# A graph stack of four layers on one core: a rewritten prelude, other buffers for the last turned rows, and attention scores of one head over all 1024 keys

## The chip, the cores and the metric

The kernel runs on one core of a Trainium2 chip. A core has five engines that work at the same time, each through its own list of instructions in order: TensorE (PE; its weight loads are PEld), VectorE (DVE), ScalarE (ACT), GpSimd (POOL), and SyncE (SP), which issues the DMA transfers here. SBUF is the memory on the core, 128 partitions wide; matmuls write to PSUM, which has eight banks of 512 float32 a partition. The metric is the time on the device of one execution, in microseconds; the median of three runs is taken.

## What is computed

x is (16, 1024, 64) float32: 16 elements of 1024 nodes with 64 channels. adj is (16, 1024, 1024), symmetric, zeros and ones, about 1.6% ones, heavier towards the first nodes. Four layers are added to x one after another, each on a normalized copy:

```
h = relu(layernorm(x)); x += quantiles(h, dilate(adj)) -> two-layer MLP
h = relu(layernorm(x)); x += (adj + I) @ h / rowsum(adj + I)
h = relu(layernorm(x)); x += attention(h, adj) @ W_proj.T + b_proj
h = relu(layernorm(x)); x += adj @ (h @ W3) + b3

quantiles: dilate drops every skip-th neighbour of nodes with over 10 neighbours;
           per node and channel, over the remaining neighbours' values:
           .25 q(.25) + .5 q(.5) + .25 q(.75), linear interpolation, plus h itself
attention: 8 heads of 64; q, k, v = h @ W_qkv.T
           g0, g1 = exp(h @ W_gamma.T + b_gamma)
           softmax(g0 * (q @ k.T) / 8 + g1 * adj) @ v
```

## The kernel before

**Layer 0 by ranks.** The kernel never sorts a node's neighbours. It ranks each channel's 1024 values once, and then looks for the wanted order statistic of every node by counting. `ranked` (L942) normalizes two elements, so that 2 x 64 channels fill the 128 partitions, and `ranks` (L542) sorts those 128 rows with 55 compare-exchange steps in float32 (L577 to L579), stores the sorted values to DRAM (`vs_d`), reverses the 55 steps in float16 with masks kept in DRAM (L609 to L612) to get each value's rank, and stores the ranks to DRAM (`rk_d`). `dilate` (L470) makes the thinned neighbour masks of an element. `stages` (L1016) then prepares an element in small steps: it fetches its ranks, builds the neighbour matrix (`neighbours`, L511), the rank positions that are sought (`positions`, L627, ending with six rows `krow` that ScalarE copies), and the table of differences of sorted values (`sorted_table`, L668).

**The comparison loop.** `picks` (L779) has for every element 96 steps: 8 groups of 8 channels, 2 halves of 512 nodes, 6 order statistics. A step (`compare`, L813) is three VectorE passes over 128 x 2048 (`le` L819, `wa` L821, `wb` L823), then matmuls into `prep` and `val` (L842), then `bits` (L854) and `value` (L865). The cumulated counts that it compares come from 512-wide matmuls `px` (L735) whose results ScalarE copies several times (`group`, L713).

**The other layers.** `turned` (L1089) goes once over all 128 blocks of 128 rows of adj: load, row sums on ScalarE, transposes on TensorE (`chunk_cols`, L450), and a store of the transposed block to DRAM (`adjT`). `layer1` (L1104) and `layer3` (L1240) read such blocks back through `turned_rows` (L1099) and multiply with them (`weighted`, L1073). `layer2` (L1123) is the attention: per pair of heads, keys and queries for all nodes (`pk`, `pq`, L1166: each one matmul of 128 output rows for each 512 nodes, copied by ScalarE at L1173, both heads side by side on the partitions), values `pv2`, and then for each of 8 blocks of 128 query nodes:

```
for t in range(NH):                     # half of the keys
    sp[:, 0, :], sp[:, 1, :] = scores of both heads, 512 keys      (L1201)
    for e in range(2):                  # head
        s[e][:, t half] = ad - sp[:, e, :]; nm[e] = its minimum,   (L1210)
                          begun with nm[e] of the first half
exp of each head's 1024 (L406), transposes, eT @ v (L1224), projection (L1233)
```

The minimum is that of the negated scores, so it is the softmax's maximum. One `sp` tile of two PSUM banks exists; matmuls of a tile that are next to each other are held together by `adjoining`.

**What sets the order.** The program is written out in one list. `picks` yields a number after each of its steps, the numbers add up to an account `due`, and as long as the account is above zero the generator `layers()` is advanced, which pays back what each of its steps is worth. A comparison step pays 0.42; a block of `turned` costs 0.3; the three later layers of an element cost 40.3 together. While `picks` works on element b, `background(b + 1)` thins the next element and ranks half of the next pair, one small step for each comparison. Before the first comparison everything of element 0 has to be made: that prelude (`background(0)`, then `els[0].stages`, then the first weights) pays 0.0 for each step up to the end of the ranking and 0.05 for the first group, so that hardly anything of `layers()` lies in it. The prelude runs the ranking and the thinning in turn, two steps of the first for one of the second, and only then the stages of element 0. When `picks` has ended, `alone` is set: the last element's layers 1 to 3 are left, and other buffers are taken for some tiles.

**Constants.** Before all this, L127 to L388 make constant tiles: masks, bit-reversed index tables, selectors, weights. Their scratch memory is given back (L389) just before the pool `sb` is opened (L390), so the first loads of x wait until the last reader of it has gone by.

**Buffers.** `b4`, `b2_`, `a4`, `q4`, `tb` are tiles of SBUF by size class with some buffers each; tag `bt` has 2 buffers, shared by `chunk_cols` and `turned_rows`, `tb` has 6; in PSUM, `pa`, `pb` and `pc_` have 2 banks each.

Of the kernel before, what the change touches and what calls it, by code (L numbers as in the profile page):

```python
# [8 lines left out]
F32 = mybir.dt.float32  # L9
# [29 lines left out]
def tile_preln_adj_stack(  # L39
# [87 lines left out]
    scr_i = sc("scr_i", (P, 5, P), I32)  # L127
    scr_f = sc("scr_f", (P, 3, P))
    identf = const.tile([P, P], F32, name="identf")
    make_identity(nc, identf)  # L130
    ident = const.tile([P, P], HP, name="ident")
    nc.vector.tensor_copy(ident, identf)

    rev_i = sc("rev_i", (P, C), I32)
    nc.gpsimd.iota(rev_i, pattern=[[1, C]], base=0, channel_multiplier=C)
    rev_a = sc("rev_a", (P, C), I32)
    rev_b = sc("rev_b", (P, C), I32)
    nc.vector.memset(rev_a, 0)
    for b_ in range(N.bit_length() - 1):
        up = N.bit_length() - 2 - 2 * b_  # L140
        nc.vector.tensor_scalar(
            rev_b, rev_i, 1 << b_, abs(up), op0=OP.bitwise_and,
            op1=OP.logical_shift_left if up >= 0 else OP.logical_shift_right,
        )
        nc.vector.tensor_tensor(rev_a, rev_a, rev_b, OP.bitwise_or)
    rev = sc("rev", (P, C), HP)
    nc.vector.tensor_copy(rev, rev_a)
    rev_d = dram.tile([P, C], HP, name="rev_d")
    nc.sync.dma_start(rev_d, rev)
    minus_i = const.tile([P, P], BF, name="minus_i")  # L150
    nc.vector.tensor_scalar(minus_i, identf, -1.0, None, op0=OP.mult)
# [3 lines left out]
    fmp_i = scr_i[:, 0, :]  # L155
    nc.gpsimd.iota(fmp_i, pattern=[[1, P]], base=0, channel_multiplier=-1)
    fmp = scr_f[:, 0, :]
    nc.vector.tensor_copy(fmp, fmp_i)


    step2 = sc("step2")
    nc.vector.scalar_tensor_tensor(step2, fmp, 2.0, identf, op0=OP.is_equal, op1=OP.subtract)
    dif = const.tile([P, 2, P], HP, name="dif")
    nc.vector.tensor_scalar(dif[:, 0, :], step2, -SPAN, None, op0=OP.mult)
    nc.vector.tensor_scalar(dif[:, 1, :], step2, -1.0, None, op0=OP.mult)
    less = const.tile([P, 2, P], HP, name="less")
    nc.vector.tensor_scalar(less[:, 0, :], identf, -2.0, None, op0=OP.mult)
    nc.vector.tensor_scalar(less[:, 1, :], identf, -FINE, None, op0=OP.mult)

    prow_i = scr_i[:, 1, :]  # L170
    nc.gpsimd.iota(prow_i, pattern=[[0, P]], base=0, channel_multiplier=1)
    fcol_i = scr_i[:, 2, :]
    nc.gpsimd.iota(fcol_i, pattern=[[1, P]], base=0, channel_multiplier=0)
    par_i = scr_i[:, 3, :]


    sel_w = const.tile([P, 2, 2 * BKW], HP, name="sel_w")
    nc.vector.tensor_scalar(par_i, prow_i, 1, None, op0=OP.bitwise_and)
    par = const.tile([P, 2], F32, name="par")
    nc.vector.tensor_copy(par[:, 1:2], par_i[:, 0:1])  # L180
    nc.vector.tensor_scalar(par[:, 0:1], par[:, 1:2], -1.0, 1.0, op0=OP.mult, op1=OP.add)
    par_up = const.tile([P, 2], F32, name="par_up")
    nc.vector.tensor_scalar(par_up, par, UP, None, op0=OP.mult)
    for c2 in range(2):
        cols = slice(c2 * BKW, (c2 + 1) * BKW)
        for i, w in enumerate((2.0, 2.0 * FINE)):
            nc.vector.tensor_scalar(
                sel_w[:, i, cols], fcol_i[:, :BKW], 0.0, w, op0=OP.mult, op1=OP.add
            )
            nc.vector.tensor_scalar(sel_w[:, i, cols], sel_w[:, i, cols], par[:, c2 : c2 + 1], None, op0=OP.mult)  # L190

    def bits_reversed(x, bits, n, name):
        r, u = sc(name + "_r", (P, n), I32), sc(name + "_u", (P, n), I32)
        nc.vector.memset(r, 0)
        for i in range(bits):
            up = bits - 1 - 2 * i
            nc.vector.tensor_scalar(
                u, x, 1 << i, abs(up), op0=OP.bitwise_and,
                op1=OP.logical_shift_left if up >= 0 else OP.logical_shift_right,
            )  # L200
            nc.vector.tensor_tensor(r, r, u, OP.bitwise_or)
        return r


    pblk = scr_i[:, 3, :]
    same = scr_f[:, 1, :]
    fblk = scr_i[:, 4, :]
    nc.vector.tensor_scalar(fblk, fcol_i, 4, None, op0=OP.logical_shift_right)
    fpl = sc("fpl", (P, P), I32)
    nc.vector.tensor_scalar(fpl, fcol_i, 15, None, op0=OP.bitwise_and)  # L210
    fplr = bits_reversed(fpl, 4, P, "fpl")
    ppl = sc("ppl", (P, P), I32)
    nc.vector.tensor_scalar(ppl, prow_i, 15, None, op0=OP.bitwise_and)
    pplr = bits_reversed(ppl, 4, P, "ppl")
    nc.vector.tensor_scalar(pblk, prow_i, 4, None, op0=OP.logical_shift_right)
    nc.vector.tensor_tensor(same, pblk, fblk, OP.is_equal)

    to30 = const.tile([P, 2], I32, name="to30")
    field = sc("field", (P, P))
    nc.vector.tensor_scalar(field, pplr, 15.0, None, op0=OP.is_equal)  # L220
    keep = sc("keep", (P, P))
    nc.vector.tensor_scalar(keep, field, -1.0, 1.0, op0=OP.mult, op1=OP.add)
    nc.vector.tensor_scalar(to30[:, 0:1], pplr[:, 0:1], 15.0, keep[:, 0:1], op0=OP.add, op1=OP.mult)
    nc.vector.tensor_scalar(
        to30[:, 1:2], field[:, 0:1], -65536.0 - 1073741824.0, 1073741824.0, op0=OP.mult, op1=OP.add
# [3 lines left out]
    tri = scr_f[:, 2, :]  # L229
    nc.vector.tensor_tensor(tri, pplr, fplr, OP.is_le)  # L230
    nc.vector.tensor_tensor(tri, tri, same, OP.mult)
    nc.vector.tensor_scalar(tri, tri, 0.5, None, op0=OP.mult)
    nc.vector.scalar_tensor_tensor(tri, identf, -40.5, tri, op0=OP.mult, op1=OP.add)
    nc.vector.tensor_tensor(tri, tri, keep, OP.mult)
    nc.vector.tensor_tensor(field, field, same, OP.mult)
    nc.vector.scalar_tensor_tensor(tri, field, 1.0 / KHI, tri, op0=OP.mult, op1=OP.add)
    nc.vector.tensor_scalar(field, fplr, 15.0, -0.5, op0=OP.is_equal, op1=OP.mult)
    nc.vector.tensor_scalar(field, field, 1.0, None, op0=OP.add)
    nth = const.tile([P, P], BF, name="nth")
    nc.vector.tensor_tensor(nth, tri, field, OP.mult)  # L240
# [3 lines left out]
    nc.vector.memset(sel_t, 0.0)  # L244
    for i in range(2):
        nc.vector.tensor_tensor(sel_t[:, i, 8 * i : 8 * i + 8], pblk[:, 0:8], fcol_i[:, 0:8], OP.is_equal)

    sel_c = const.tile([P, 8], F32, name="sel_c")
    nc.vector.tensor_scalar(pblk, prow_i, 7, None, op0=OP.bitwise_and)
    nc.vector.tensor_tensor(sel_c, pblk[:, 0:8], fcol_i[:, 0:8], OP.is_equal)  # L250
# [3 lines left out]
    fbk = sc("fbk", (P, P), I32)  # L254
    nc.vector.tensor_scalar(fbk, fcol_i, 1, None, op0=OP.logical_shift_right)
    pbk = sc("pbk", (P, P), I32)
    nc.vector.tensor_scalar(pbk, prow_i, 63, None, op0=OP.bitwise_and)
    pbkr = bits_reversed(pbk, 6, P, "pbk")
    for e in range(2):
        nc.vector.tensor_tensor(tab_d[:, e, :], fbk, pbkr, OP.is_equal)  # L260
    nc.vector.tensor_scalar(pbkr, pbkr, 1.0, None, op0=OP.add)
    fnx = sc("fnx", (P, P))
    nc.vector.tensor_tensor(fnx, fbk, pbkr, OP.is_equal)
    nc.vector.tensor_scalar(pbk, prow_i, 6, None, op0=OP.logical_shift_right)
    for e in range(2):
        nc.vector.tensor_tensor(tab_d[:, e, :], tab_d[:, e, :], fnx, OP.subtract)
        ph_ = sc("ph_", (P, P))
        nc.vector.tensor_scalar(ph_, pbk, float(e), None, op0=OP.is_equal)
        nc.vector.tensor_tensor(tab_d[:, e, :], tab_d[:, e, :], ph_, OP.mult)
# [4 lines left out]
    nc.vector.memset(none, 0.0)  # L274
    ones = const.tile([P, P], BF, name="ones")
    nc.vector.memset(ones, 1.0)

    k16 = const.tile([P, NBK, 2], HP, name="k16")
    nc.vector.tensor_scalar(
        k16.rearrange("p b s -> p (b s)"), fbk, 16.0, 15.0, op0=OP.mult, op1=OP.add  # L280
    )

    prow = sc("prow", (P, 1))
    nc.vector.tensor_copy(prow, prow_i[:, 0:1])
    off = sc("off", (P, 2))
    bkt = sc("bkt", (P, 1), I32)
    nc.vector.tensor_scalar(bkt, prow_i[:, 0:1], 1, None, op0=OP.logical_shift_right)
    nc.vector.tensor_scalar(off[:, 0:1], bkt, 8.0, -SHIFT, op0=OP.mult, op1=OP.add)
    nc.vector.tensor_scalar(off[:, 1:2], bkt, 0.0, None, op0=OP.is_equal)
    shifts = const.tile([P, 6], F32, name="shifts")  # L290
    nc.vector.tensor_scalar(
        shifts[:, 0:1], off[:, 0:1], -1.0, None, op0=OP.mult
    )
    nc.vector.tensor_scalar(
        shifts[:, 1:2], off[:, 0:1], -SPAN, None, op0=OP.mult
    )
    first = (FIRST - SHIFT) * SPAN / FINE
    rest_ = 8.0 * SPAN / FINE
    nc.vector.tensor_scalar(
        shifts[:, 2:3], off[:, 1:2], first - rest_, rest_, op0=OP.mult, op1=OP.add  # L300
    )
    nc.vector.tensor_scalar(shifts[:, 3:4], shifts[:, 2:3], FINE, None, op0=OP.mult)
    nc.vector.memset(shifts[:, 4:5], -0.5)
    nc.vector.memset(shifts[:, 5:6], 2.0 * (160.0 - FIRST) + 2.0)

    def at_row(dst, terms):

# [203 lines left out]
    def neighbours(left_d, rem_d, t):  # L511
# [3 lines left out]
        for j in range(C):  # L515
# [22 lines left out]
            if j < C - 1:  # L538
                yield None
        yield valid  # L540

    def ranks(V):  # L542

# [775 lines left out]
```

## Time and profile before

| | |
|---|---|
| median of 3 runs | 12626.17 us (12620.15 to 12635.34) |
| the profiled execution itself | 12620.06 us |
| its span | 12618.3 us, 217315 instructions |
| ScalarE busy | 9465.7 us (75%) |
| chain that ended last, by engine | PE 6%, ACT 3%, DVE 2% of the span |
| DMA | 908.21 MB, mean 72 GB/s |

The profile is of one execution, whose own time is 12620.06 us: 1.8 us of it lie outside the span. The page lists for each engine its busy time and number of instructions (the "x" figures), and then groups of instructions: line, engine, operation, output and inputs with their sizes, count, total busy us and mean ns of one, then the idle time of the engine just before such instructions and what ended most of it. A table by stage gives, for each stretch of time, each engine's busy time and count, the clock granted to TensorE, the busy share of the DMA engines and their GB/s. The chain that ended last covers only an eighth of the span here, so it says little of this kernel. A timeline row is start, duration, engine, line, operation, and in square brackets a wait that it ended; a row that stands for several equal instructions ("x4") has its first start and the time to the last end.

### The profile page before, as it was taken

The page shows a single profiled execution, that of the slowest core. Times are in us where ns is not written, and L with a number is a line of the kernel's source. Part 1 is how long each engine was busy: PE and PEld are TensorE (multiplying, and loading weights), DVE is VectorE, ACT ScalarE, POOL GpSimd, SP SyncE. Part 2 cuts the span into 40 slices and gives each one's busy share as a digit, 9 for nine tenths or more (in the row PEclk, how much of TensorE's full clock was granted, in tenths as well). Part 3 has the DMA queues.
Part 4 walks back from the last instruction along what each step waited for, and adds up shares of the span by engine and source line. Part 5 has one row for each costly group of instructions (what it writes and reads, how often), then busy time and mean ns, then how long its engine had stood idle before and what let it go on. Part 6 is the DMA issues. An engine that isn't in the chain of part 4 may idle for free. (4 is left out here: it accounts for less than half of the span.)

```text
span 12618.3 us, 217315 instructions
## 1 busy us (share of the span) xinstructions
PE 11271.0 (89%) x84666; PEld 5355.3 (42%) x84673; DVE 11557.3 (92%) x19682; ACT 9465.7 (75%) x17018; POOL 1.4 (0%) x10
## 2 busy tenths in 40 slices
PE   0888999999899998999989999999999999999988
PEld 0334444444444444444444444444444444444445
DVE  8899989999899999989999899999989999988873
ACT  0897877777777777777877777777777777787866
POOL 0000000000000000000000000000000000000000
PEclk9999999999999999999999999999999999999989
DMA  3672121221212122121211212112121211201011
GB/s 105 219 248 82 56 75 52 71 65 57 71 53 82 55 63 65 54 79 56 71 57 56 78 56 75 54 61 71 55 77 53 72 62 57 88 30 56 31 52 60
DMA packets 521609, 908.21 MB, mean 72 GB/s; under 512 B 240768, under 2 KB 275712, under 8 KB 520576
## 3 DMA queue, kind: packets, MB, share of 16 engines
q1 hardware_dynamic: 520576, 894.31, 21.9%
q8 instruction: 663, 10.86, 0.4%
q14 instruction: 370, 3.03, 0.1%
HBM read 683.38 MB, written 206.57 MB: 71 GB/s over the span
## 5 line engine op out<-in xcount | busy, mean ns | idle before, releaser
L821 DVE TENSOR_TENSOR wa<-le,c 128x2048 f16<-128x2048 f16 x1536 | 1868.8, 1217 | 189.4 <-PE prep L842 127.7
L735 PE MATMUL px<-valid,cw 128*128 128x512 fp8e4 x8192 | 1964.9, 381 | 0.0
L823 DVE TENSOR_TENSOR wb<-le,c 128x2048 f16<-128x2048 f16 x1536 | 1866.9, 1215 | 0.0
L819 DVE TENSOR_TENSOR le<-cum,krow 128x2048 f16<-128x2048 int16 x1536 | 1862.5, 1213 | 2.9 <-ACT cum L406 2.3
L406 ACT ACTIVATE c<-px,shifts 128x512 f16<-128x512 f32 x2048 | 1428.1, 700 | 258.4 <-PE px L762 126.1
L406 ACT ACTIVATE s<-s,nm 128x1024 f32<-128x1024 f32 x1024 | 1171.5, 1147 | 243.1 <-DVE nm L1210 230.1
L735 PEld LDWEIGHTS <-cw 128*128 128x128 f16 x8192 | 799.2, 98 | 1133.1 <-issue 240.1
L459 PE MATMUL pcols<-identf,s 128*128 128x128 f32 x8192 | 1177.8, 281 | 112.5 <-ACT eT L462 49.1
L1201 PE MATMUL sp<-kT,qT 64*128 64x512 f32 x4096 | 1163.5, 641 | 62.8 <-DVE nm L1210 61.3
L869 DVE SCALAR_TENSOR_TENSOR vs<-pz,vs 128x512 f32<-128x512 f32 x1536 | 1047.2, 682 | 148.4 <-PE pz L862 110.4
L459 PEld LDWEIGHTS pcols<-identf,s 128*128 128x128 f32 x8192 | 906.1, 142 | 641.3 <-ACT eT L462 273.4
L849 ACT COPY wi<-prep 128x512 f32<-128x512 f32 x1536 | 913.0, 594 | 347.1 <-PE prep L842 315.6
L842 PE MATMUL val<-le,tab 128*32 128x512 f16 x12288 | 1147.6, 390 | 23.6 <-ACT wi L849 13.1
L462 ACT COPY eT<-pcols 128x512 f32<-128x512 f32 x2048 | 1133.1, 603 | 26.2 <-PE pcols L459 24.8
L406 ACT ACTIVATE high<-px,shifts 128x512 f16<-128x512 f32 x1024 | 712.9, 696 | 582.4 <-PE px L735 577.4
L1224 PE MATMUL ao<-eT,v 128*64 128x128 f32 x16384 | 1071.4, 276 | 21.8 <-ACT eT L462 20.2
L406 ACT ACTIVATE vs<-val 128x512 f32<-128x512 f32 x1536 | 939.5, 612 | 192.1 <-PE val L842 117.5
L1224 PEld LDWEIGHTS ao<-eT,v 128*64 128x64 f32 x16384 | 903.8, 137 | 278.2 <-ACT eT L462 153.7
L842 PE MATMUL prep<-wb,sel_w 128*32 128x512 f16 x6144 | 664.6, 396 | 214.4 <-DVE wb L823 204.7
L1210 DVE CUSTOM_DVE_ANT_0 s<-sp,ad,nm 128x512 f32<-128x512 f32 x1024 | 725.9, 744 | 122.7 <-PE sp L1201 122.6
L857 DVE TENSOR_SCALAR bit<-wi,to 128x512 int32<-128x512 int32 x1536 | 827.0, 538 | 3.6 <-ACT cw L406 2.8
L1210 DVE CUSTOM_DVE_ANT_0 s<-sp,ad 128x512 f32<-128x512 f32 x1024 | 683.3, 682 | 121.7 <-PE sp L1201 112.3
(271 smaller groups left out, 18163.5 us busy)
## 6 DMA issues: line engine op xcount, KB each, us to landing
ad<-in_adj_dram SPq DMA_DIRECT2D x768, 512.0 KB
aT<-adjT SPq DMA_DIRECT2D x256, 512.0 KB
adjT<-aT SPq DMA_DIRECT2D x128, 512.0 KB
md<-sm SPq DMA_DIRECT2D x216, 256.0 KB
sb<-md SPq DMA_DIRECT2D x216, 256.0 KB
rem_d<-rem SPq DMA_DIRECT2D x128, 256.0 KB
left_d<-nb SPq DMA_DIRECT2D x128, 256.0 KB
lr<-left_d SPq DMA_DIRECT2D x256, 128.0 KB
```

The source lines that it names most:

```text
L406: nc.scalar.activation(out_, in_, func, **kw)
L459: nc.tensor.transpose(pt[:, c, :], ad[:, (4 * s + c) * P : (4 * s + c + 1) * P], identf)
L462: nc.scalar.copy(aT[:, 4 * s : 4 * s + 4, :], pt)
L735: yield nc.tensor.matmul(px[pp], w[:, j, :], valid[:, j, :], start=False, stop=j == C - 1, skip_group_check=True,)
L819: nc.vector.tensor_tensor(le, cum, bc(el.krow[q][:, None, hs], [P, 4, 512]), OP.is_lt)
L821: nc.vector.tensor_tensor(wa, le, c0, OP.mult)
L823: last = nc.vector.tensor_tensor(wb, le, c1, OP.mult)
L842: yield nc.tensor.matmul(dst[32 * pp : 32 * pp + 32, :], w[pp], r[pp], start=i == 2, stop=i in (1, 3), tile_position=(0, 32 * pp), skip_gr ...
L869: nc.vector.scalar_tensor_tensor(vs, pz, 80.0, vs, op0=OP.is_equal, op1=OP.mult)
L1201: nc.tensor.matmul(sps[e], qT[e * D : (e + 1) * D, i * P : (i + 1) * P], kT[e * D : (e + 1) * D, hs], start=True, stop=True,)
L1210: nc.vector.tensor_tensor_reduce(ss[e][:, hs], sps[e], ad[:, hs], -1.0, 3.0e38 if t == 0 else nms[e], op0=OP.add, op1=OP.min, accum_out=nm,)
L1224: nc.tensor.matmul(ao[e * D : (e + 1) * D, :], v[:, j, e * D : (e + 1) * D], eTs[e][:, j, :], start=j == 0, stop=j == C - 1, tile_position ...
```

## The change

It has four parts.

1. **Constants.** The same constant tiles are made in another way: index patterns come from GpSimd's iota, columns of one number a partition take the place of full 128 x 128 tiles, and casts and scalings go to ScalarE. VectorE has 88 instructions there instead of 235. The store of the reversal table `rev_d` moves from the beginning to the end of the constants.
2. **First prelude.** Each step of `background(0)` pays 0.07 instead of 0.0, so `turned` blocks are issued within it: in the built program 30 of 128 blocks stand before the first comparison, and all 128 before the 65th. The stages of element 0 are put into the same round as soon as the thinning has ended, beside the ranking, instead of after it. For element 0 the ranks are copied directly from PSUM instead of being stored and fetched back, and its `vs`, `u` and `df` tiles take other buffers.
3. **Turned rows.** When `alone` is set, `turned_rows` takes its tile from `tb` (6 buffers) instead of `bt` (2).
4. **Scores.** A head's keys are kept as [128, 2, 512]: the lower 64 partitions have keys 0 to 511, the upper 64 have keys 512 to 1023, one column range for each head. Each query is kept on both partition halves, for 512 nodes at a time; the second 512 are made when block 4 begins. One head's scores over all 1024 keys fill the two banks of `sp`, and one reduction of 128 x 1024 takes them, with no earlier minimum to begin from. When `alone` is set, the second head's scores go to two separate banks and are reduced in two steps of 512. Of the 2048 reductions 992 of 1024 keys and 64 of 512 remain; of 256 matmuls of 64 x 512 for keys and queries (128 output rows each) there become 768 of 64 output rows each (256 for keys, 512 for queries), and ScalarE's copies of queries go from 128 to 256.

The core of the diff, the constants cut to an example:

```diff
-    rev_i = sc("rev_i", (P, C), I32)
-    nc.gpsimd.iota(rev_i, pattern=[[1, C]], base=0, channel_multiplier=C)
...
-    for b_ in range(N.bit_length() - 1):
...
-    nc.sync.dma_start(rev_d, rev)
...
+    rev_c = iota("rev_c", [(128, 2), (256, 2), (512, 2)])
...
+    ident = scaled("ident", (P, P), HP, identf, 1.0)
...
+    rev = sc("rev", (P, C), HP)
+    nc.vector.tensor_scalar(rev, rev_c, rv[:, 6:7], None, op0=OP.add)
...
-    nc.vector.memset(wproj, 0.0)
+    nc.gpsimd.memset(wproj, 0.0)
...
+    nc.sync.dma_start(rev_d, rev)
     scr.close()
...
         for r in background(0):
-            yield 0.0
+            yield 0.07
...
     def ranks(V, own):
...
+        if own is not None:
+            own.rk = place("rk")
+            nc.scalar.copy(own.rk, pt[:, :, :D])
         rs = b2_("rs", (P, C, P), HP)
...
             except StopIteration:
                 going.remove(gen)
+                if b == 0 and gen is thinning:
+                    going.append(els[0].stages)
                 continue
...
-        el.rk = sb.tile([P, C, D], HP, tag="rk", bufs=2, name="rk")
-        nc.sync.dma_start(el.rk, rk_d[:, :, rows])
-        yield
+        pair = pairs[b // 2]
+        if b:
+            el.rk = place("rk")
+            nc.sync.dma_start(el.rk, pair[2][:, :, rows])
+            yield
...
-        vs = q4("vs")
-        nc.sync.dma_start(vs[rows, :], vs_d[rows, :])
+        while not pair:
+            yield
+        mine = q4 if b else a4
+        vs = mine("vs")
+        nc.sync.dma_start(vs[rows, :], pair[1][rows, :])
...
     def turned_rows(b, i, name):
-        aT = sb.tile([P, C, P], F32, tag="bt", bufs=2, name=name)
+        aT = (
+            tb(name, (P, C, P), F32) if alone
+            else sb.tile([P, C, P], F32, tag="bt", bufs=2, name=name)
+        )
...
+            def queries(s, keys):
...
+                for r in range(2):
+                    pk, pq = pb("pk") if keys else None, pb("pq")
...
+                        for n in range(2):
+                            half = slice(n * D, (n + 1) * D)
+                            if keys:
+                                yield nc.tensor.matmul(
+                                    pk[half, :], wqkv[:D, (2 * pr + r) * D : (2 * pr + r + 1) * D],
+                                    hT[:D, n * 512 : (n + 1) * 512], start=True, stop=True,
+                                    tile_position=(0, n * D), skip_group_check=True,
+                                )
+                            hd = 2 * pr + n ^ r
+                            yield nc.tensor.matmul(
+                                pq[half, :], wqkv[D:, hd * D : (hd + 1) * D], hT[D:, hs],
+                                start=True, stop=True, tile_position=(D, n * D), skip_group_check=True,
+                            )
...
+                    adjoining(made())
+                    if keys:
+                        nc.scalar.copy(kT[:, r, :], pk)
+                    nc.scalar.copy(q[:, r, :], pq)
...
+            qT = queries(0, True)
...
             for i in range(C):
+                if i == C // 2:
+                    qT = queries(1, False)
...
-                for t in range(NH):
-                    hs = slice(t * 512, (t + 1) * 512)
-                    if alone and t % 2:
-                        sps = [pc_("sp") for _ in range(2)]
+                cols = slice(i % 4 * P, (i % 4 + 1) * P)
+                for e in range(2):
+                    if alone and e:
+                        sps = [pc_("sp") for _ in range(NH)]
                     else:
-                        sp = ps.tile([P, 2, 512], F32, tag="sp", bufs=1, name="sp")
-                        sps = [sp[:, e, :] for e in range(2)]
+                        sp = ps.tile([P, NH, 512], F32, tag="sp", bufs=1, name="sp")
+                        sps = [sp[:, t, :] for t in range(NH)]
                     adjoining(
                         nc.tensor.matmul(
-                            sps[e], qT[e * D : (e + 1) * D, i * P : (i + 1) * P],
-                            kT[e * D : (e + 1) * D, hs], start=True, stop=True,
+                            sps[t], qT[t * D : (t + 1) * D, t ^ e, cols],
+                            kT[t * D : (t + 1) * D, e, :], start=True, stop=True,
                         )
-                        for e in range(2)
+                        for t in range(NH)
                     )
-                    for e in range(2):
+                    if alone and e:
+                        parts = [(sps[t], slice(t * 512, (t + 1) * 512)) for t in range(NH)]
+                    else:
+                        parts = [(sp.rearrange("p t k -> p (t k)"), slice(0, N))]
+                    for s, hs in parts:
...
                         nc.vector.tensor_tensor_reduce(
-                            ss[e][:, hs], sps[e], ad[:, hs], -1.0, 3.0e38 if t == 0 else nms[e],
+                            ss[e][:, hs], s, ad[:, hs], -1.0, nms[e] if hs.start else 3.0e38,
                             op0=OP.add, op1=OP.min, accum_out=nm,
                         )
```

## The prediction

> **What bounds the kernel now.** I read the page first, then the busy time by stage (cut at the first compare of each element), then the waits and the timelines of the edited places.
>
> ```profile
> PE 11271.0 (89%) x84666; PEld 5355.3 (42%) x84673; DVE 11557.3 (92%) x19682; ACT 9465.7 (75%) x17018; POOL 1.4 (0%) x10
> ...
> L1210 DVE CUSTOM_DVE_ANT_0 s<-sp,ad,nm 128x512 f32<-128x512 f32 x1024 | 725.9, 744 | 122.7 <-PE sp L1201 122.6
> ...
> L1210 DVE CUSTOM_DVE_ANT_0 s<-sp,ad 128x512 f32<-128x512 f32 x1024 | 683.3, 682 | 121.7 <-PE sp L1201 112.3
> ```
> VectorE looks like the bound, TensorE close behind. By stage (stretch; length; then PE, PEld, DVE, ACT, POOL busy; clock; DMA):
>
> ```profile
> 0.00:349.10 349.10, 46.74 (x202) 22.23 (x203) 285.08 (x799) 59.02 (x91) 1.35 (x10) 0.98 0.33 102
> 349.10:1007.80 658.70, 564.50 (x3887) 256.37 (x3887) 615.40 (x845) 599.83 (x1097) 0.00 (x0) 0.98 0.69 237
> ...
> 1741.80:2517.40 775.60, 706.01 (x5235) 330.51 (x5235) 731.57 (x1195) 577.34 (x1034) 0.00 (x0) 0.98 0.20 64
> 10081.10:10820.40 739.30, 683.64 (x5206) 323.01 (x5206) 704.71 (x1235) 572.83 (x1025) 0.00 (x0) 0.98 0.20 64
> 10820.40:11543.20 722.80, 679.05 (x5245) 323.35 (x5243) 627.28 (x999) 571.94 (x1034) 0.00 (x0) 0.98 0.17 54
> 11543.20:12232.60 689.40, 648.33 (x5010) 303.06 (x5008) 579.97 (x886) 528.58 (x960) 0.00 (x0) 0.98 0.12 38
> 12232.60:12618.30 385.70, 321.75 (x2464) 217.06 (x2460) 131.12 (x348) 223.97 (x443) 0.00 (x0) 0.86 0.22 69
> ```
> These are prelude, element 0, 2 (even), 13 (odd), 14, 15, tail. Element 14 is a free experiment: 77 us less VectorE work than 13, the same TensorE work, and only 16.5 us shorter. So TensorE with its waits needs about 723 us an element. VectorE's work plus idle is 739 odd, 775 even. An odd element has only 16 us of room before TensorE binds; 14, 15 and the tail are TensorE's already.
>
> **One reduction over 1024 keys.** 1984 of the 2048 reductions become 992 (the last element's second heads keep two each). What one takes of VectorE is read from start to next start:
>
> ```profile
> 4404.69 0.68 DVE L1210 CUSTOM_DVE_ANT_0 s<-sp,ad 128x512 f32<-128x512 f32 x1
> 4405.30 0.07 DVE L1210 DVE_READ_ACCUMULATOR2_ANT nm<- 128x1 f32 x1
> 4405.30 2.28 DVE L483 TENSOR_TENSOR_SCAN cumn<-nb 128x1024 f16<-128x1024 bf16 x1
> ...
> 4410.98 0.73 DVE L1210 CUSTOM_DVE_ANT_0 s<-sp,ad,nm 128x512 f32<-128x512 f32 x1
> 4411.65 0.08 DVE L1210 DVE_READ_ACCUMULATOR2_ANT nm<- 128x1 f32 x1
> 4411.65 1.22 DVE L821 TENSOR_TENSOR wa<-le,c 128x2048 f16<-128x2048 f16 x1
> ```
> The halves take 0.61 and 0.67 us; the accumulator read starts with the next instruction, so it is free. Another 512 elements cost 0.54 us (f32 TENSOR_TENSOR at 128x1024, L697, 1.23 us, against 0.69 at 128x512). A whole row is 0.61 + 0.54 = 1.15 us; saved 1.28 - 1.15 = 0.13 us a head, 8.3 us an element (64 heads). The row's means would give 0.68 + 0.74 - 1.22 = 0.20, 13 an element: they count overlapped tails. The Trainium skill (Perfetto Trace Analysis, Optimizing Scalar/DVE Operations) puts the overhead of a VectorE instruction on PSUM at about 0.125 us of engine time, half its profiled latency: 8.0 an element. I take 8.3.
>
> **What it costs TensorE.** The halves of a head must sit on both row halves, so each query is made twice, in 64x64 tiles, the second half at i = 4: 12 matmuls a pair of heads for 4, and 6 ScalarE copies for 4 (L1173, 0.587 us each: 2 x 4 x 0.587 = 4.7 us an element on ScalarE, which has 160 spare). Today:
>
> ```profile
> 4408.22 1.13 PE L1201 MATMUL sp<-kT,qT 64*128 64x512 f32 x4 [0.83 <-DVE nm L1210]
> 4409.28 0.39 PE L756 MATMUL px<-low,dif 128*128 128x512 f16 x1
> ...
> 5019.22 1.12 PE L1166 MATMUL pk<-h2T,wqkv 64*128 64x512 f32 x2
> 5019.91 1.12 PE L1166 MATMUL pq<-h2T,wqkv 64*128 64x512 f32 x2
> 5020.97 0.40 PE L862 MATMUL pz<-bit,nth 128*128 128x512 bf16 x1
> ```
> Two f32 matmuls on different rows share 1.06 us when nothing lies between (sp); pk and pq wait for separate PSUM buffers and take 1.75 here, 1.25 or 2.1 elsewhere, mean 1.7, so 3.4 a pair of heads. Column tiles overlap too (prep L842: four in 0.23 us); all four quadrants at once no row shows. New: 2 x 1.75 with keys + 2 x 1.06 without = 5.6, so +2.2 a pair, +9 an element. Bounds: perfect overlap 4 x 1.06 = 4.2 (+3.4 an element); no overlap 24 passes x 0.53 = 12.7 (+37). I take +9, nearest to the pk/pq row. Both score matmuls still come per round, two rounds an i, so the waits on sp stay; ScalarE's exp of the first head can start earlier. At i = 4 the copies wait for the scores of i = 3, and sp and its reduction wait for them (some 1.5 us); other VectorE work usually stands between. I add nothing, at most 6 us an element.
>
> Per element: odd, VectorE 739 - 8 = 731 against TensorE 723 + 9 = 732: about 733 from 737, -4. Even: 775 - 8, -7 with a little induced waiting. Seven odd (1 to 13), six even: -28 - 42 = -70. Elements 14 and 15: +8 each. Sum -54. Another rule speaks for more: the same page (Identifying the Most-Contended Engine) judges TensorE by its weight loads, not its matmul busy time; at 44% (323 of 739) it has headroom, and then 8.3 passes whole through 15 elements: -125. Element 14 says no; I follow the row.
>
> **Constants.** Before the mask's conversion VectorE runs 235 instructions, in the built program of the new kernel 88. The loads of x reuse the scratch memory: issued at 24.19, just after the last scratch read (23.58). At 23.6/235 = 0.10 us each, with a wait for the iotas, the 88 end near 12. GpSimd's extra iotas and memsets (0.1 to 0.3 each) and ScalarE's casts lie beside them; only the projection weights wait for a GpSimd memset. Two degree passes (1.1 us) now precede the norm's Sqrt on ScalarE: +2, less the table load (1.28) taken earlier. Net -11 (-5 to -14).
>
> **First prelude.** Its waits:
>
> ```profile
> DVE m L640 <- PE pm L637: 18.4, 1, 18.4
> DVE ve L427 <- ACT sq L406: 17.5, 3, 15.2
> DVE tab L695 <- ACT df L406: 7.5, 1, 7.5
> ```
> The ranking ends at 286.1, the first compare starts at 349.1: 63 us, of which 318.1 to 349.1 goes from the first weights to the compare; in that stretch ten krow copies take 6.1 us of ScalarE. Masks, tables and krow now run beside the ranking, and the ranks come by a copy, not through DRAM: 1.3 + 31 - 6 = 26, so -37. Their ten VectorE instructions (5.8 us) move into the ranking: +5, since some fill its 0.03 us gaps. 30 of 128 turned blocks come into the prelude in the built order, 1 MB of traffic each, some 120 GB/s on top of 102; element 0 bears 237. On SP their stores wait for ScalarE with mask stores and fetches of the ranking behind; one fetch cost 3.2 us today. +6 (0 to 25). Net -26.
>
> **Element 0.** Turning ends two thirds through, not at the end. VectorE idles 43 us of 659, mostly behind TensorE: a third of it is 14; I take -10 (0 to -25).
>
> **Tail.** Turned rows: TensorE takes 3.02 us a block at half clock (two 1.98, copy, po 0.69) and waits for ScalarE only, never for a load; more buffers give 0 (-2 to +5: three loads wait on SP for compare buffers with element 14's last blocks behind). TensorE is 92% busy in the middle, so the queries add 4 x 2.2 = 9; +10.
>
> **Sum.** -11 - 26 - 10 - 54 + 10 = -91 on the span of 12618.3 (this execution 12620.06, 6 under the median): 12626 - 91 = **12,535**.
>
> **Rivals.**
> (1) Whole gain: VectorE alone paces and the tiles overlap: -125 for the elements, -40 prelude, -15 element 0: 12,446. For: the rule above, the even elements. Against: element 14. 0.22.
> (2) TensorE eats it: at x = 18 us extra an element the odd ones take 741 (+3 each, +21), even -35, elements 14, 15 and tail +54, against -47: about 12,620, no change. 0.14.
> (3) Slower: the 64x64 tiles run one after another, +37: odd 760 (+22 x 7), even +5 x 6, the rest +111, -47: +248, 12,874. It decides from some 20 us an element, 5 a pair. Against: rows and columns overlap separately in the trace. 0.10.
> Mine 0.54, spread 12,450 to 12,600.
>
> Faster by over 0.2% (25 us, about what a measurement can tell) 0.76, within 0.14, slower 0.10. Range 12,420 to 12,645.
>
> **What would show it.** Reduction near 1.22 us and 1056 of them; if 1.35 or more, the cut is gone. Odd elements near 733, even 768, 14 near 731. The pk/pq busy union per element: about twice today's is right, four times is rival 3. First compare near 312; much later means SP or DMA stalls inside the ranking. Tail near 395.

## The result, and the profile after

The changed kernel takes 12510.04 us (median of five runs; 12498.93 to 12511.81), against 12626.17 us before: a ratio of 0.9907, 95% interval 0.9892 to 0.9921. The forecast was 12,535, so the gain came out at 116 instead of 91. The profiled execution has a span of 12504.6, 113.7 less than before.

The page of the changed kernel, first the engines' busy time, then two groups kept apart by shape:

```profile
PE 11332.3 (91%) x85683; PEld 5376.8 (43%) x85697; DVE 11411.9 (91%) x17538; ACT 9572.4 (77%) x17160; POOL 3.2 (0%) x20
```
```profile
L1224 DVE CUSTOM_DVE_ANT_0 s<-sp,ad 128x1024 f32<-128x1024 f32 x992 | 1209.6, 1219 | 258.8 <-PE sp L1211 254.9 <-ACT s L379 1.3 <-ACT eT L435 1.0
...
L1224 DVE CUSTOM_DVE_ANT_0 s<-sp,ad 128x512 f32<-128x512 f32 x32 | 22.1, 691 | 35.0 <-PE sp L1211 35.0
```
The whole-row reduction takes 1219 ns, where two halves had means of 682 and 744. VectorE has 145 us less work, TensorE 61 us more, and the two are level. VectorE's wait ahead of the reductions has not fallen (122.7 + 121.7 before, 294 now). By stage, cut as for the kernel before (the tail begins with the last comparison): prelude, element 0, 2 (even), 13 (odd), 14, 15, tail:

```profile
0.00:307.84 307.84, 113.78 (x498) 73.55 (x499) 266.33 (x643) 144.32 (x253) 3.20 (x20) 0.65 0.72 241
307.84:958.20 650.36, 543.83 (x3593) 225.81 (x3593) 615.75 (x844) 530.68 (x950) 0.00 (x0) 0.98 0.53 181
1696.30:2458.20 761.90, 701.74 (x5298) 328.22 (x5298) 722.60 (x1066) 581.68 (x1042) 0.00 (x0) 0.98 0.20 65
9940.50:10675.50 735.00, 686.31 (x5269) 323.21 (x5270) 697.21 (x1108) 578.26 (x1034) 0.00 (x0) 0.98 0.21 65
10675.50:11400.60 725.10, 684.30 (x5308) 324.31 (x5307) 618.85 (x871) 580.28 (x1042) 0.00 (x0) 0.98 0.17 54
11400.60:12086.80 686.20, 649.75 (x5074) 303.66 (x5072) 571.22 (x758) 536.21 (x968) 0.00 (x0) 0.98 0.13 40
12086.80:12504.60 417.80, 333.23 (x2528) 218.27 (x2524) 128.52 (x284) 232.75 (x451) 0.00 (x0) 0.87 0.18 60
```
VectorE's work in element 2 fell from 731.6 to 722.6 and in 13 from 704.7 to 697.2, as worked out (8.3). The lengths did not all follow. Cut in the same way for all elements, the change on the span is:

| stage | forecast | measured |
|---|---|---|
| prelude | -37 | -41.3 |
| element 0 | -10 | -8.3 |
| odd elements 1 to 13 | -28 | -18.7 |
| even elements 2 to 12 | -42 | -76.6 |
| elements 14 and 15 | +16 | -0.9 |
| tail | +10 | +32.2 |
| sum | -91 | -113.7 |

So the total is near by luck and not for the reasons of the forecast: the even elements gave nearly twice what was expected, the tail took three times as much.

### The profile page after: what moved, and what is told of

Its sections match the earlier page's. It is cut to its first block, busy times and chain, and to the rows that moved or that the text cites. A ratio compares the mean times of both kernels' runs of the same rounds, so it can differ in the third digit from the quotient of the medians.

```text
span 12504.6 us, 216870 instructions
## 1 busy us (share of the span) xinstructions
PE 11332.3 (91%) x85683; PEld 5376.8 (43%) x85697; DVE 11411.9 (91%) x17538; ACT 9572.4 (77%) x17160; POOL 3.2 (0%) x20
## 5 line engine op out<-in xcount | busy, mean ns | idle before, releaser
L802 DVE TENSOR_TENSOR wb<-le,c 128x2048 f16<-128x2048 f16 x1536 | 1872.1, 1219 | 0.0
L1224 DVE CUSTOM_DVE_ANT_0 s<-sp,ad 128x1024 f32<-128x1024 f32 (+1 forms) x1024 | 1231.5, 1203 | 293.8 <-PE sp L1211 289.9
L1211 PE MATMUL sp<-kT,qT 64*128 64x512 f32 x4096 | 1230.9, 643 | 38.5 <-DVE nm L1224 35.9
L821 PE MATMUL val<-le,tab 128*32 128x512 f16 x12288 | 1110.1, 389 | 23.8 <-ACT wi L828 13.7
L848 DVE SCALAR_TENSOR_TENSOR vs<-pz,vs 128x512 f32<-128x512 f32 x1536 | 1052.1, 685 | 83.4 <-PE pz L841 78.0
L379 ACT ACTIVATE vs<-val 128x512 f32<-128x512 f32 x1536 | 939.7, 612 | 110.2 <-PE val L821 72.4
L841 PE MATMUL pz<-bit,nth 128*128 128x512 bf16 x1522 | 611.1, 402 | 176.7 <-DVE bit L836 116.4
```

The costliest lines, as they stand in the source:

```text
L379: nc.scalar.activation(out_, in_, func, **kw)
L802: last = nc.vector.tensor_tensor(wb, le, c1, OP.mult)
L821: yield nc.tensor.matmul(dst[32 * pp : 32 * pp + 32, :], w[pp], r[pp], start=i == 2, stop=i in (1, 3), tile_position=(0, 32 * pp), skip_gr ...
L848: nc.vector.scalar_tensor_tensor(vs, pz, 80.0, vs, op0=OP.is_equal, op1=OP.mult)
L1211: nc.tensor.matmul(sps[t], qT[t * D : (t + 1) * D, t ^ e, cols], kT[t * D : (t + 1) * D, e, :], start=True, stop=True,)
L1224: nc.vector.tensor_tensor_reduce(ss[e][:, hs], s, ad[:, hs], -1.0, nms[e] if hs.start else 3.0e38, op0=OP.add, op1=OP.min, accum_out=nm,)
```

## The experiments

The theory on trial: VectorE's shorter reductions are worth what the engine that paces a stage lets through; TensorE, with dearer queries, paces odd elements, 14, 15 and the tail. Rivals: TensorE has room everywhere; the order of steps matters more than either engine's work; the tail's loss is due to the turned rows. Stage lengths are from each run's profiled execution (odd: mean of elements 1 to 13; even: 2 to 12):

| run | first compare | element 0 | odd | even | 14 | 15 | tail | ratio to before, interval |
|---|---|---|---|---|---|---|---|---|
| before | 349.1 | 658.7 | 737.4 | 775.1 | 722.8 | 689.4 | 385.7 | 1 |
| the change | 307.8 | 650.4 | 734.7 | 762.3 | 725.1 | 686.2 | 417.8 | 0.9907 (0.9892, 0.9921) |
| scores_undone | 308.9 | 643.8 | 738.6 | 774.4 | 722.8 | 688.4 | 384.0 | 0.9951 (0.9936, 0.9966) |
| scores_only | 348.1 | 672.2 | 734.3 | 762.4 | 723.6 | 686.9 | 421.7 | 0.9958 (0.9943, 0.9973) |
| halves | 309.9 | 652.6 | 745.8 | 766.9 | 728.0 | 691.3 | 419.1 | 0.9992 (0.9983, 1.0000) |
| queries_twice | 312.9 | 642.7 | 746.6 | 762.4 | 739.6 | 702.4 | 414.7 | 0.9995 (0.9986, 1.0004) |
| tail_old | 312.5 | 650.5 | 734.0 | 762.8 | 723.4 | 686.2 | 387.6 | 0.9881 (0.9866, 0.9896) |
| queries_early | 309.8 | 642.6 | 734.7 | 762.2 | 724.1 | 686.6 | 418.4 | 0.9908 (0.9892, 0.9925) |
| queries_ahead | 309.7 | 652.7 | 734.7 | 762.5 | 723.5 | 684.9 | 408.5 | 0.9900 (0.9886, 0.9915) |
| turn_later | 306.8 | 664.1 | 734.0 | 762.9 | 723.4 | 686.5 | 422.5 | 0.9919 (0.9904, 0.9933) |
| queries_copied | 310.1 | 643.1 | 731.1 | 760.6 | 721.3 | 682.6 | 432.3 | 0.9877 (0.9862, 0.9892) |
| tail_ahead | 312.4 | 652.5 | 734.6 | 762.9 | 723.0 | 686.7 | 384.7 | 0.9885 (0.9871, 0.9900) |
| best | 310.3 | 646.1 | 730.7 | 761.1 | 719.0 | 681.8 | 384.7 | 0.9846 (0.9830, 0.9863) |

Where a stage's code is the same, odd and even means, 14 and 15 repeat within 2 us; the first comparison scatters by 5 (307.8 to 312.9 in the ten runs with the whole new prelude, mean 310.4) and element 0 by 10 (642.6 to 652.7 there, mean 647.7; 658.7 and 672.2 in the two runs with the old prelude), so a difference of a few us in these says nothing.

**scores_undone**: the changed kernel with `layer2` of the kernel before.

```diff
-                for e in range(2):
...
+                for t in range(NH):
```


> The changed kernel with layer 2 as it was before (512-key reductions of both heads, queries made once); constants, prelude and turned rows stay changed. My theory, that the scores alone move the elements and the tail: even elements back at 775, odd near 738, 14 and 15 at 723 and 689, the tail back at 386 from 418, prelude and element 0 as in the changed kernel (308 and 650). Sum: 12504.6 + 96 (elements 1 to 15) - 32 (tail) = 12569 on the span. Rival, the turned rows' buffers lengthen the tail: it stays near 418, 12601. Rival, the even elements gained by another order of their steps that the prelude brought: they stay near 762, 12485 to 12500.

The elements and the tail went back (even 774.4, tail 384.0) and the prelude kept its gain. The span is 12564.3. The turned rows' buffers are worth at most 2 us, in either direction.

**scores_only**: the reverse, the kernel before with the new `layer2`.

```diff
-                for t in range(NH):
...
+            def queries(s, keys):
...
+                for e in range(2):
```


> The kernel before with nothing but the new layer 2. My theory: prelude and element 0 as before (349 and 659), even elements 762 to 763, odd 733 to 738, 14 and 15 at 725 and 686, tail 418. Sum 12618.3 - 96 + 32 = 12554 on the span. Rival, the parts hang together (turning that is done earlier makes room for the scores): even elements stay near 770 and the sum is above 12590.

Elements and tail have the new lengths, and the two parts are independent as far as the scatter shows: the spans fell by 54.0 and 50.8 alone, and by 113.7 together. The span (12567.5) is 13 above the expectation, all of it in element 0 (672.2), whose code is unchanged here (658.7 in the run of before).

**halves**: each row of 1024 is reduced in two steps from the same tile.

```diff
-                    if alone and e:
+                    if e or not alone:
                         parts = [(sps[t], slice(t * 512, (t + 1) * 512)) for t in range(NH)]
```


> The changed kernel with every score row of 1024 reduced in two steps of 512 from the same tile, in elements 1 to 14: layout, queries and order stay new, only VectorE's work comes back (8.5 us an element). My theory: even elements 762 + 7 to 9 = 770, odd ones 735 + 3 to 8, 14 and 15 nearly unmoved (under 3), in all 12505 + 95 = 12600. Rival, the even elements gained by the new order (a head's scores and its exp come together) and not by VectorE's shorter work: they stay at 762 to 765, in all under 12545.

VectorE's work came back (element 2: 732.0, element 13: 705.4), and with layout, queries and order still new this run cuts the change to the scores in two (its profiled execution took 12625.00 us, 12 more than the median of its twelve, so that its elements may stand some 0.8 us too long here):

| mean of an element | before | new layout and queries (halves) | and whole rows (the change) |
|---|---|---|---|
| odd | 737.4 | 745.8 (+8.4) | 734.7 (-11.1) |
| even | 775.1 | 766.9 (-8.2) | 762.3 (-4.6) |
| 14 | 722.8 | 728.0 (+5.2) | 725.1 (-2.9) |
| 15 | 689.4 | 691.3 (+1.9) | 686.2 (-5.1) |

Odd elements pay 8.4 for the new layout and queries, and get 11.1 back for 8.3 of VectorE work. Even ones gain from the new layout alone, though TensorE has more matmuls to do and VectorE the same work. Neither my expectation nor the rival had both. The waits of VectorE in element 2 show where it comes from, the kernel before and then this one (total us, times, longest):

```profile
DVE vs L869 <- PE pz L862: 8.7, 5, 3.2
DVE o L1068 <- PE y L1064: 8.3, 1, 8.3
DVE wa L821 <- PE prep L842: 5.2, 3, 3.2
DVE vs L869 <- ACT aoT L1231: 4.9, 1, 4.9
```
```profile
DVE o L1053 <- PE y L1049: 8.3, 1, 8.3
DVE wa L800 <- PE prep L821: 7.5, 5, 3.2
...
DVE vs L848 <- PE pz L841: 2.2, 3, 1.3
```
The comparison loop's last step (`value`, L848 now) waited 13.6 us, 4.9 of it behind the attention's copy `aoT`, and waits 2.2 now; VectorE's whole idle time fell from 44 to 35. Why `value` waited is seen in TensorE's own order. In these places of the kernel before, the eight `val` matmuls of a comparison step (L842, 0.60 us elsewhere) are issued in turn with the second half of a block's `ao` matmuls, and `pz`, for which `value` waits, stands behind both (TensorE's rows, then VectorE's):

```profile
1936.31 1.09 PE L1224 MATMUL ao<-eT,v 128*64 128x128 f32 x16
1937.34 0.39 PE L842 MATMUL val<-le,tab 128*32 128x512 f16 x1
1937.66 0.43 PE L1224 MATMUL ao<-eT,v 128*64 128x128 f32 x2
...
1942.11 0.39 PE L842 MATMUL val<-le,tab 128*32 128x512 f16 x1
1942.43 0.43 PE L1224 MATMUL ao<-eT,v 128*64 128x128 f32 x2
1942.79 0.40 PE L862 MATMUL pz<-bit,nth 128*128 128x512 bf16 x1
```
```profile
1943.23 0.69 DVE L869 SCALAR_TENSOR_TENSOR vs<-pz,vs 128x512 f32<-128x512 f32 x1 [3.22 <-PE pz L862]
```
The traces give how often this happens in each odd or even element, and how long `value` waits there in all (mean us):

| places with `val` and `ao` in turn, wait of `value` | before | halves | the change | queries_twice | queries_copied |
|---|---|---|---|---|---|
| odd | 0, 3.0 | 1, 5.1 | 0, 1.8 | 0, 2.1 | 0, 2.0 |
| even | 3, 13.7 | 0, 1.9 | 1, 4.6 | 0, 2.2 | 1, 4.4 |

So the order of a few matmuls is a part of both columns of the table above. Of the 11.1 that whole rows gave the odd elements, 3.3 are these waits, and of the 8.4 that the new layout cost them, 2.1; in the even ones whole rows gave 4.6 although these waits rose by 2.7. Without them whole rows are worth about 7.8 and 7.3 (an estimate, from the two tables), for 8.3 and 9.4 of VectorE work.

**queries_twice**: a dose of TensorE work and nothing else.

```diff
+                            for _ in range(1 if alone else 2):
                                 yield nc.tensor.matmul(
                                     pq[half, :], wqkv[D:, hd * D : (hd + 1) * D], hT[D:, hs],
```


> The changed kernel with every query matmul of elements 0 to 14 issued twice into the same place: about 15 us more of TensorE an element, nothing more on the other engines. My theory as forecast, that TensorE with its waits paces elements 14 and 15 and is close behind VectorE in the others: 14 and 15 longer by 13 to 15 each, odd ones by 8 to 13, even ones by 3 to 8; in all 12505 + 150 = 12655 on the span (prelude, element 0 and tail stay). Rival, that TensorE has room and only VectorE's work and the order of the waits count: all of them by less than 4, in all under 12560.

The busy union of the key and query matmuls rose by 14 us in an odd element (20.8 to 35.0), 16.5 in an even one, 14 in elements 14 and 15. Odd elements took 11.9 of it, 14 and 15 took 14.5 and 16.2, even ones nothing on balance (762.4; 3 to 8 was expected), with 2.4 less of the waits of `value`. An even element (2), and 14, which was the reason for the forecast's bound, in this run:

```profile
1701.40:2464.90 763.50, 707.74 (x5361) 331.25 (x5362) 723.17 (x1066) 581.49 (x1042) 0.00 (x0) 0.98 0.20 65
...
10756.60:11496.10 739.50, 696.01 (x5371) 328.19 (x5370) 620.13 (x871) 579.16 (x1042) 0.00 (x0) 0.99 0.17 53
```
The weight loads (PEld) fill 43% and 44% of these stretches. By the rule that the forecast set aside, to judge TensorE by them (the Trainium skill, Perfetto Trace Analysis, Identifying the Most-Contended Engine; the page wants its share of peak work too, which was not worked out here), it would have room in both; it has in the even one alone. So time on TensorE does lengthen the odd elements, 14 and 15, and in the even ones some 14 of the 16.5 us are hidden. The added matmuls stand ahead of a pair's scores: whether the engine has no time left or its later results are waited for, this run alone does not tell.

**queries_copied**: as many 128-column matmuls as before the change, and ScalarE puts the heads on the partition halves.

```diff
-                            yield nc.tensor.matmul(
-                                pq[half, :], wqkv[D:, hd * D : (hd + 1) * D], hT[D:, hs],
...
+                    yield nc.tensor.matmul(
+                        both[1], wqkv[D:, pr * P : (pr + 1) * P], hT[D:, hs], start=True, stop=True
+                    )
...
+                        for m in range(2):
+                            nc.scalar.copy(q[m * D : (m + 1) * D, 1, :], pq[(1 - m) * D : (2 - m) * D, :])
```


> The changed kernel, but keys and queries are made by as many 128-column matmuls as before the change, and ScalarE brings each head to the partition halves by copies of 64 partitions (40 copies of about 0.6 us an element for 24). My theory, that TensorE paces the odd elements, 14 and 15, and not the even ones: key and query matmuls fall from 20.8 to about 15 us an element, odd elements from 735 to 729 to 731, 14 and 15 by 4 to 6 each, even ones stay at 762; the last element's tail gains nothing or loses a few us to the added copies. In all 12505 - 45 = 12460 on the span. Rival, ScalarE's longer copies ahead of the scores take the gain back: odd elements stay at 734 to 738, in all 12500 or more.

The union in odd elements fell from 20.8 to 15.9. Odd elements fell by 3.7, 14 and 15 by 3.8 and 3.6, even ones by 1.7, together 44; ScalarE's 10 us more cost the elements nothing. The tail, where nothing covers the copies, lost 14.5. In all 12470.32.

**tail_old, queries_early, queries_ahead, tail_ahead**: four versions of the last element.

```diff
-        yield from layer2(b, xr)
+        yield from (layer2_old if alone else layer2)(b, xr)
```


> The changed kernel, but the last element, whose layer 2 has no comparisons beside it, uses the scores of before. My theory: the tail is 386, all else is as in the changed kernel: 12504.6 - 32 = 12473 on the span. Rival, the turned rows' buffers are what lengthens the tail: it stays near 418 and the span near 12505.

The tail is back at 387.6, with the new buffers for turned rows in place: the scores alone lengthened it. Why shows in what TensorE waited for in one pair of heads of the tail, first before (65.7 us), then changed (74.8 us):

```profile
PE pp L1233 <- ACT aoT L1231: 3.6, 7, 0.6
PE sp L1201 <- DVE nm L1210: 0.6, 1, 0.6
PE pcols L459 <- ACT eT L462: 0.4, 1, 0.4
```
```profile
PE ao L1238 <- ACT eT L435: 3.3, 3, 2.1
PE pcols L432 <- ACT s L379: 3.3, 5, 1.2
PE pp L1247 <- ACT aoT L1245: 1.4, 4, 0.4
PE pcols L432 <- ACT eT L435: 0.9, 2, 0.7
```
Before, the next block's scores stand between and fill the time in which ScalarE works on a block's exponentials and copies. TensorE's rows around block 4 of the changed kernel:

```profile
12274.94 1.96 PE L1238 MATMUL ao<-eT,v 128*64 128x128 f32 x30
12277.31 0.49 PE L1247 MATMUL pp<-wproj,aoT 128*128 128x128 f32 x2 [0.41 <-ACT aoT L1245]
12277.73 1.93 PE L1170 MATMUL pq<-h2T,wqkv 64*64 64x512 f32 x8
12279.59 0.69 PE L1211 MATMUL sp<-kT,qT 64*128 64x512 f32 x1
```
The second queries come after the last projection (`pp`) of block 3, with which they share a pair of PSUM banks in turn, and only then come the scores of block 4; the last scores ahead of them were at 12264.54. For 15 us no score is made, and VectorE, with nothing to reduce, is busy for 1.04 of the 10 us from 12269. A pair of heads has two such places now instead of one. At the second the granted clock was 0.67 here (12309.0 to 12313.8), and 1.00 at the same place before (12438.6 to 12443.4); the changed kernel's third pair had 1.00 there too and still took 73.3 us, so the clock is a small part of the loss at most.

Making the second queries when the pair begins:

```diff
             qT = queries(0, True)
+            later = queries(1, False) if alone else None
```


> The changed kernel, but in the last element both halves of the queries are made when a pair of heads begins, the second half in a tile of its own. My theory: the 22 us of the tail that I had not forecast are the pipeline of blocks running dry when block 4 begins, since the new scores wait for queries whose PSUM bank comes after the results of block 3 in turn; without it the tail is 386 + 9 to 14 for the doubled queries = 395 to 400, 12485 on the span. Rival, the two separate banks and two-part reduction of each second head break the rhythm of the blocks: the tail stays above 410.

The step from block 3 to block 4 (between their copies `att`) fell from 16.2 us to 6.4, but the step after it rose from 5.1 to 9.1, and the tail stayed at 418.4: at the pair's start keys and queries now take 13.7 us from first to last in the first pair, and 7.9 in the others, where nothing covers them, and VectorE starts later. What I expected of this run fell: the cost moved.

```diff
+                if i == (C // 2 - 2 if alone else C // 2):
+                    later = queries(1, False)
```


> The changed kernel, but in the last element the second half of the queries is made two blocks ahead, into a tile of its own and from the PSUM banks of the second head's scores, so that it isn't behind the results of block 3. Moving them to the start of a pair only moved their cost there. My theory, the dry pipeline at block 4: the step from block 3 to 4 falls from 16.2 us to 8 or less, the tail from 418 to 418 - 4 x 8 = 386 to 392. Rival, the time is lost all over the blocks: the step falls but the tail stays above 405.

The step fell to 6.4 as well, but the one after it is again 9.1, the one from block 1 to block 2, where the queries now stand, rose from 11.3 to 14.4, and the tail fell only to 408.5, as the rival said. In a pair, 65.7 us before, 74.8 in the changed kernel and 70.4 here, TensorE's busy time is 62.2 for 60.6 before, and its idle time 8.2 for 5.1. Before, most blocks of a pair followed one another by 7.5 us; in the new arrangement the steps go from 4.5 to 12.2 us even in queries_early, where no queries are made between the blocks. So moving the queries gets back some 9 of the 32 us, and 21 to 25 are lost in all of the new arrangement: busier TensorE (6 us in four pairs) and its added idle time (12), part of it waits for a single head's exponentials (3.3 us in this pair). What else breaks the rhythm no run here separates.

With the scores of before, the next pair's keys, queries and values ahead of time:

```diff
+                if i == C // 2 and pr < H // 2 - 1:
+                    ready = made_for(pr + 1, pc_)
```


> The changed kernel with the scores of before in the last element, and there keys, queries and values of the next pair of heads made while block 4 of the present pair is at work, from the PSUM banks of the scores. My theory, that the tail pays for a TensorE that stands dry where queries are made: the 19.4 us between the last block of a pair and the first of the next fall to about 12, three times; the tail from 387 to about 365, the span from 12475 to 12453. Rival, the tail is bound by its chain of blocks: it stays at 380 or more.

The 19.4 us between two pairs fell to 7.5, but a step of 15.3 appeared at block 4, where the new matmuls now stand; the tail is 384.7, hardly better than tail_old. In the tail the dry place goes where keys and queries are made.

**turn_later**:

```diff
         for r in background(0):
-            yield 0.07
+            yield 0.0
```


> The changed kernel, but the steps of the first prelude pay nothing, so that no turned block is issued beside the ranking. My theory: turned blocks cost the prelude 6 us (the wait for the reversal table behind their transfers, the mask fetches) and save element 0 some 10: first comparison at 301, element 0 at 660, in all 12505 + 4 = 12509. Rival, the turned blocks cost the prelude nothing: first comparison stays at 308, in all 12515.

The first comparison came at 306.8, 1 us ahead of the changed kernel's profile and 3.6 ahead of the mean of the ten runs; element 0 took 664.1, 16 more than their mean. Turned blocks cost the prelude somewhat less than I had said and save more, and the whole is 11 us slower without them (12520.95 against 12510.04, and the fastest of its four runs, 12518.20, is above the slowest of the changed kernel's five).

**best**: queries_copied for elements 1 to 14 and tail_ahead for the last, both edits as above.

> The two together: copied queries in elements 1 to 14, the scores of before with the next pair ahead in the last. If each does what it should, 12505 - 45 - 52 = 12408 on the span; if neither does, 12475.

12430.30: faster than both kernels, and faster than the changed one by about the sum of what the two gave alone (44 in the elements, 33 in the tail). The other 20 us that were expected of the tail are missing, as in tail_ahead.

## Why the prediction came out right

- **Reductions** (0.13 us a head, 8.3 an element): right. The tail's timeline has whole rows 1.14 to 1.15 us from start to next start; 1.15 was worked out. VectorE lost 7.5 to 9.0 an element.
- **Queries** (+9 us of TensorE an element): +7.0 in their own union (13.8 to 20.8) and +4 in `sp` (72.4 to 76.5), close to the sum. The third rival, that the tiles run one after another, is out: three times as many matmuls, each of half the output rows, took one and a half times the time.
- **Odd elements** (-4 each): -2.7, the right size by two larger terms: +8.4 and -11.1. The step "about 733" took the later of two engines, 731 and 732. The runs show that in these elements both engines' work counts at once: 14 us more of TensorE cost 11.9, and 8.3 less of VectorE saved 11.1, of which 3.3 are the waits of `value`. So the lengths are not a maximum of two sums; that the engines alternate, one waiting for the other, fits this and is not shown step by step.
- **Even elements** (-7 each): the failed step, -12.8. It had 8 us of VectorE's work and "the waits on sp stay", and 1 us of extra waiting. The waits on sp did stay, but others went: the layout and order alone are worth 8.2 (halves), and the shorter work 4.6. The waits that vanished are those of `value` behind `val` and `ao` in turn: three such places in each even element before, one in the changed kernel, none in halves (13.7, 4.6 and 1.9 us of waiting). VectorE's work was worth about what the forecast gave it (7.3, by the estimate above); what the forecast had at nothing is this order. The amount of query work does not decide it, since queries_twice has no such place and queries_copied one; which part of the new layout moves the places, no run here separates, and it stays open.
- **Elements 14 and 15** (+8 each): more time on TensorE lengthens them, as said (queries_twice), but they ended at +2.3 and -3.2. The price was 5.2 and 1.9 where the forecast had 8, and VectorE's shorter work gave 2.9 and 5.1 back, which the forecast had put at nothing.
- **Prelude** (-37): -41.3. The constants end 12.5 earlier (27.27 to 14.80 at the mask's conversion; -11 was forecast); the ranking's backward half is 12 longer (5 + 6 forecast, but of it 5.4 is VectorE's added work and 3.6 a longer wait for the table `rev_d`, 4.6 us for 1.0, of which turn_later, with 3.4, shows most to come from something else than turned blocks); from the ranks to the first comparison it is 23 instead of 63 us (-37 forecast). **Element 0**: -8.3 for -10, within its scatter; by turn_later against the mean, 16.
- **Tail** (+10): +32. The queries were charged at 4 x 2.2; that they stand in turn behind the projection, so that the pipeline of blocks empties twice a pair, was considered for the middle ("some 1.5 us", at i = 4) and left out of the tail, where no comparison covers it. The turned rows gave nothing, as said.

Two errors of 35 and 22 had opposite signs; without them the sum would have been the same to within 13. That they nearly cancel is luck. Of the rivals, the whole gain (12,446) comes nearest in the even elements, and what the second (TensorE eats it, at 18 us an element) would have been is seen in queries_twice: with 21 us more of key and query matmuls in an odd element than before the change it took 12616.71, no gain worth the name, and 12,620 was worked out.

## What to carry to other kernels

Where two engines wait for each other, the length of a stage need not be the larger of two sums: give the stage a dose of each engine's work and see what passes through, before a saving on one is paid for with work on the other. An edit that is judged in the busy middle has to be judged again in the part where nothing runs beside it; the same code was worth -13 us in an even element and +32 in the last one. Before a gain or a loss of a few us is put down to an engine's work, count the places where two groups of matmuls are issued in turn: the waits at three of them were longer in an even element here than what the shorter reductions saved. If a new step takes a buffer in turn behind the results of the step before, the work ahead of it can no longer be brought forward, and moving the step mostly moves the gap.

## What the runs showed of the hardware that was not expected

Float32 matmuls of 64 rows by 64 columns on all four quarters of the array share time: four of them with 512 columns of data took 1.50 us (keys and queries together, 12313.84 to 12315.34), while two on different rows take 1.06. The granted clock of TensorE in the new prelude was 0.65, where it had been 0.98 with less work (114 us busy, 47 before); it cost the sort's forward half nothing, since VectorE set the pace there: it takes 143.8 us at a granted clock of 0.53, and 144.1 before at 1.00, with no matmuls beside it.
